# Swapping the two DMA issuers of a matrix-per-sample residual kernel: ScalarE for the loads, SyncE for the stores

## The chip, the core and the metric

The kernel runs on one core of a Trainium2 chip. The metric is the device time of one execution in microseconds (us). Before the change it is 326.86 us, the median of 3 runs (326.13 to 327.13). The profile is one further execution of the same program, taken by the hardware profiler; its span is 325.4 us.

## What is computed

There are 128 samples. Each has a matrix x[b] of 128 channels by 1024 steps, and an index that picks one of eight 128 by 128 weight matrices. The picked matrix, transposed, is multiplied with x[b], and x[b] is added to the product. All numbers are 32-bit floats.

```python
# x: (128, 128, 1024) f32; itok_B_0_7: (128,) int32 in 0..7; L0_cond_weights: (8, 128, 128) f32
def reference(x, itok_B_0_7, L0_cond_weights):
    w = L0_cond_weights[itok_B_0_7]
    return x + jnp.einsum('bct,bcd->bdt', x, w)
```

So 67.11 MB of x are read and 67.11 MB of output are written, beside 0.52 MB of weights and 512 bytes of indices.

## The kernel before

The work goes in 32 tiles of four samples (`NT`, with `G * H = 4`), and a tile in two pairs of samples (`j` counts the 64 pairs). Twelve tiles of x fit into SBUF at once (`SLOTS`, the buffers `x0` to `x11`, 2 MB each); tile i uses buffer i modulo 12. The output is written over x in its buffer and stored from there, so a buffer comes free when its store has landed.

Everything is in one hand-ordered block (`tc.tile_critical()`, line 139). Each engine runs its own list of instructions in the written order, and the lists meet only at semaphores:

- SyncE (line 161 to 169) first loads all eight matrices into `w_all`, then each sample of x by its own DMA of 512 KB, four for a tile. From tile 12 on it waits, before the first load of a tile, until the buffer's earlier store has landed (lines 165 and 167; this is called a slot wait below).
- ScalarE first loads the subjects, that is the 128 indices (line 141). Then it has one store for each tile, of 2 MB, made by `store` (line 130), and before each of them a wait until VectorE has added the tile (`s_added`, line 222). The first tile is stored in two halves, the last tile as one pair and two single samples. ScalarE does no arithmetic in this kernel.
- VectorE clears `zeros`, clamps the indices (lines 153 to 157), and then adds product and x for each pair (line 217, 128 by 2048 elements in one instruction).
- GpSimd (POOL in the profile) loads the indices into registers, sixteen at a time, and copies for each sample the picked matrix out of `w_all` into one of four buffers `w` (line 196). The copy of a pair's first sample also waits until the pair's x has landed and until its PSUM buffer is free.
- TensorE (PE) warms up with products of zeros (line 146) and then makes four products for each pair, two for each sample (line 206), into one of two PSUM buffers `ps`.

`transfer` (line 50) makes each DMA of x and of the output directly, on the hardware queue of the engine that it is given (`QUEUES`, line 47), so the engine in the call settles which queue carries the bytes. A load reads a sample's 512 KB as 32 rows of 16 KB of DRAM; a store of several samples reads two samples' rows together, 8 KB for each partition.

At the end of the block all engines meet on SyncE (its instructions of line 139). A second block (lines 227 to 230) then waits on SyncE for all stores that are still on their way, and ScalarE issues the very last store, sample 127, outside both blocks (line 231), so that the framework's own end of the program waits for that one. Lines 253 and 262 stand for the opening and the closing of the program.

Of the kernel before, what the change touches and what calls it, by code (L numbers as in the profile page):

```python
# [30 lines left out]
G = 2  # L31
H = 2
# [3 lines left out]
SLOTS = 12  # L36
# [5 lines left out]
DMA = 16  # L42
# [7 lines left out]
def transfer(nc, engine, out, in_):  # L50

    later, nc._always_lower_symbolic_ap = nc._always_lower_symbolic_ap, False
    ins, outs = engine.lower_ap_dma(in_), engine.lower_ap_dma(out)
    nc._always_lower_symbolic_ap = later
    return engine.add_instruction(  # L57
        mybir.InstDMACopy(
            name=nc.get_next_instruction_name(),
            engine=engine.engine,  # L60
            ins=ins,
            outs=outs,
            mode="Copy",
            cce_op=ALU.bypass,
            queue=QUEUES[engine.engine],
        )
    )


@with_exitstack  # L70
def kernel(
    ctx: ExitStack,
    tc: tile.TileContext,
    x: bass.AP,
    subjects: bass.AP,
    weights: bass.AP,
    out: bass.AP,
):
    nc = tc.nc
    B, C, T = x.shape  # L80
    S, _, D = weights.shape
    NT = B // (G * H)

    def sbuf(name, *shape, dtype=F32):
        return ctx.enter_context(nc.sbuf_tensor(name, list(shape), dtype)).ap()

    given, near, wrap, index = (
        sbuf(name, 1, B, dtype=I32) for name in ("given", "near", "wrap", "index")
    )
    w_all = sbuf("w_all", C, S, D)  # L90
    ws = [sbuf(f"w{i}", C, 1, D) for i in range(W_SLOTS)]
    zeros = sbuf("zeros", C, N)
    xs = [sbuf(f"x{i}", C, H * G, T) for i in range(SLOTS)]
    ps = [
        ctx.enter_context(nc.psum_tensor(f"ps{i}", [D, G, T], F32)).ap() for i in range(P_SLOTS)
    ]

    s_given = tc.alloc_semaphore("s_given")
    s_wall = tc.alloc_semaphore("s_wall")
    s_index = tc.alloc_semaphore("s_index")  # L100
    s_zeros = tc.alloc_semaphore("s_zeros")
    s_copied = tc.alloc_semaphore("s_copied")
    s_product = tc.alloc_semaphore("s_product")
    s_added = tc.alloc_semaphore("s_added")

    s_pair = [[tc.alloc_semaphore(f"s_pair{i}_{h}") for h in range(H)] for i in range(SLOTS)]


    s_first = tc.alloc_semaphore("s_first")

    def emptied(i, h):

        turns = i // SLOTS
        return (DMA * G + (DMA if h == H - 1 else 0)) * turns

    def loaded(i, q):

        h = q // G
        return s_pair[i % SLOTS][h], emptied(i, h) + DMA * G

    def load(engine, i, q):
        k, h = i % SLOTS, q // G
        transfer(
            nc,
            engine,
            xs[k][:, q, :],
            x[i * H * G + q].rearrange("(a r) t -> a (r t)", r=ROWS),
        ).then_inc(s_pair[k][h], DMA)

    def store(i, q0, q1):  # L130
        k, b = i % SLOTS, i * H * G
        transfer(
            nc,
            nc.scalar,
            out[b + q0 : b + q1].rearrange("g d t -> d g t"),
            xs[k][:, q0:q1, :].rearrange("d (o g) t -> d o (g t)", g=min(G, q1 - q0)),
        ).then_inc(s_first if i == 0 and q1 == G else s_pair[k][(q1 - 1) // G], DMA)

    with tc.tile_critical():  # L139

        nc.scalar.dma_start(given, subjects.rearrange("(o b) -> o b", o=1)).then_inc(s_given, DMA)

        nc.vector.memset(zeros, 0.0).then_inc(s_zeros, 1)  # L143
        nc.tensor.wait_ge(s_zeros, 1)
        for _ in range(IDLE):
            nc.tensor.matmul(  # L146
                ps[P_SLOTS - 1][:, G - 1, :N], zeros[:, :D], zeros, start=True, stop=True
            )

        nc.vector.wait_ge(s_given, DMA)
        nc.vector.tensor_scalar(near, given, -S, S - 1, ALU.max, ALU.min).then_inc(s_index, 1)  # L153
        nc.vector.wait_ge(s_index, 1)
        nc.vector.tensor_scalar(wrap, near, 0, S, ALU.is_lt, ALU.mult).then_inc(s_index, 1)  # L155
        nc.vector.wait_ge(s_index, 2)
        nc.vector.tensor_tensor(index, near, wrap, ALU.add).then_inc(s_index, 1)  # L157
        nc.gpsimd.wait_ge(s_index, 3)


        nc.sync.dma_start(w_all, weights.rearrange("s c d -> c s d")).then_inc(s_wall, DMA)  # L161
        for i in range(NT):
            k = i % SLOTS
            if i == SLOTS:
                nc.sync.wait_ge(s_first, DMA)
            if i >= SLOTS:
                nc.sync.wait_ge(s_pair[k][H - 1], emptied(i, H - 1))
            for q in range(H * G):
                load(nc.sync, i, q)


        for j in range(NT * H):
            i, q0, q1 = j // H, j % H * G, (j % H + 1) * G
            k = i % SLOTS
            p = ps[j % P_SLOTS]

            ahead = j < P_SLOTS
            if ahead:  # L180
                nc.tensor.wait_ge(*loaded(i, q0))
            for q in range(q0, q1):
                b = i * H * G + q
                if b % R == 0:
                    _, subject = nc.values_load_multi_w_load_instructions(
                        index[0:1, b : b + R],
                        engines=[mybir.EngineType.Pool],
                        min_val=0,
                        max_val=S - 1,
                        skip_runtime_bounds_check_because="the index is clamped on the chip above",  # L190
                    )
                if b == 0:
                    nc.gpsimd.wait_ge(s_wall, DMA)
                if not ahead and q == q0:
                    nc.gpsimd.wait_ge(s_added, j - P_SLOTS + 1)
                copy = nc.gpsimd.tensor_copy(  # L196
                    ws[b % W_SLOTS], w_all[:, bass.ds(subject[b % R], 1), :]
                )
                if not ahead and q == q0:
                    copy.wait_op(*loaded(i, q0), "sem-ge")  # L200
            copy.then_inc(s_copied, 1)

            nc.tensor.wait_ge(s_copied, j + 1)
            for q in range(q0, q1):
                for t in range(0, T, N):
                    mm = nc.tensor.matmul(  # L206
                        p[:, q % G, t : t + N],
                        ws[(i * H * G + q) % W_SLOTS][:, 0, :],
                        xs[k][:, q, t : t + N],
                        start=True,  # L210
                        stop=True,
                    )
            mm.then_inc(s_product, 1)

            mine = xs[k][:, q0:q1, :]
            nc.vector.wait_ge(s_product, j + 1)
            nc.vector.tensor_tensor(  # L217
                mine, p, mine, ALU.add
            ).then_inc(s_added, 1)

            if i == 0 or q1 == H * G or i == NT - 1:
                nc.scalar.wait_ge(s_added, j + 1)
                store(i, q0 if i in (0, NT - 1) else 0, q1 - (b == B - 1))

    with tc.tile_critical() as waits:
        for i in range(NT - SLOTS, NT):
            nc.sync.wait_ge(s_pair[i % SLOTS][H - 1], emptied(i + SLOTS, H - 1))
        nc.sync.wait_ge(s_pair[(NT - 1) % SLOTS][0], emptied(NT - 1 + SLOTS, 0) + DMA)  # L230
    last = nc.scalar.dma_start(out[B - 1], xs[(NT - 1) % SLOTS][:, H * G - 1, :])

    tc.add_manual_dep(
        last.ins,
        waits.name,
        mybir.DependencyInfo(mybir.DependencyClass.NoSync, mybir.DependencyReason.SCHED_ONLY),
        reason="the end of the program waits for it",
    )
# [27 lines left out]
```

## Time and profile before

| | |
|---|---|
| median of 3 runs | 326.86 us (326.13 to 327.13) |
| the profiled execution, span | 325.4 us |
| busy: PE, VectorE, GpSimd | 241.1, 147.9, 34.3 us |
| moved by DMA | 134.85 MB, 414 GB/s over the span |
| a product, 128x512 (line 206) | 512 of them, 607 ns each |
| an addition, 128x2048 (line 217) | 64 of them, 2292 ns each |
| a load of x: issue to landing, median | 32.3 us |
| a 2 MB store: issue to landing, median | 47.3 us |
| slot waits of SyncE for stores | 78.5 us, 10 times, the longest 9.8 us |

PE is TensorE, DVE is VectorE, ACT is ScalarE, SP is SyncE; a q behind an engine's name means its sequencer, which issues DMAs and waits. A row of 40 digits cuts the span into equal slices of 8.1 us, and each digit is a busy share in tenths (9 is 90% or more). In the queue table the columns are packets, megabytes, and the time that the packets took as a share of all 16 DMA engines over the span. In a table by stretches, each row gives the stretch, its length, the busy time of PE, weight load, DVE and POOL with the number of instructions, the granted TensorE clock, the busy share of the DMA engines (over 1.00 where packets overlap a little) and GB/s. In a timeline a row gives start, duration, engine, line, operation, what it writes and reads, and how many instructions it covers.

The issue of a DMA is short where its queue has room and lasts until there is room where it has none; the transfer itself goes on after it, and its landing is told by the semaphore.

### The profile page before, as it was taken

The page shows a single profiled execution, that of the slowest core. Times are in us where ns is not written, and L with a number is a line of the kernel's source. Part 1 is how long each engine was busy: PE and PEld are TensorE (multiplying, and loading weights), DVE is VectorE, ACT ScalarE, POOL GpSimd, SP SyncE. Part 2 cuts the span into 40 slices and gives each one's busy share as a digit, 9 for nine tenths or more (in the row PEclk, how much of TensorE's full clock was granted, in tenths as well). Part 3 has the DMA queues.
Part 4 walks back from the last instruction along what each step waited for, and adds up shares of the span by engine and source line. Part 5 has one row for each costly group of instructions (what it writes and reads, how often), then busy time and mean ns, then how long its engine had stood idle before and what let it go on. Part 6 is the DMA issues. An engine that isn't in the chain of part 4 may idle for free.

```text
span 325.4 us, 1606 instructions
## 1 busy us (share of the span) xinstructions
PE 241.1 (74%) x518; PEld 95.2 (29%) x518; DVE 147.9 (45%) x68; POOL 34.3 (11%) x132
## 2 busy tenths in 40 slices
PE   6999988988888888888888888888888689000000
PEld 2444332333333333333333333333333233000000
DVE  1375754555555555454555555554554544200000
POOL 1011111011111111111011111111111010000000
PEclk9999999999999999999999999999999889655555
DMA  6999999999999999999999999999999999999994
GB/s 250 413 418 421 428 425 422 420 428 427 426 421 427 429 415 427 424 431 423 423 435 417 416 432 424 428 417 428 433 419 424 418 437 415 429 425 427 426 428 201
DMA packets 16074, 134.85 MB, mean 414 GB/s; under 512 B 2625, under 2 KB 3650, under 8 KB 3906
## 3 DMA queue, kind: packets, MB, share of 16 engines
q1 hardware_dynamic: 7184, 67.64, 49.7%
q10 hardware_dynamic: 8882, 67.11, 49.1%
q8 instruction: 4, 0.07, 0.1%
q14 instruction: 4, 0.03, 0.0%
HBM read 67.63 MB, written 67.11 MB: 414 GB/s over the span
## 4 chain that ended last, share of the span: by engine, by line
PE 42%; DVE 20%; issue 16%; POOL 4%; DMA 2%; POOLq 1%; SPq 0%
PE ps L206 42%; DVE x L217 20%; POOL w L196 4%; DMA x<-in_x_dram 2%; POOLq L196 1%; SPq L57 0%; SPq L161 0%; POOLq L139 0%; SPq L262 0%; SPq L139 0%
## 5 line engine op out<-in xcount | busy, mean ns | idle before, releaser
L206 PE MATMUL ps<-x,w 128*128 128x512 f32 x512 | 236.1, 607 | 33.6 <-POOL w L196 32.1
L217 DVE TENSOR_TENSOR x<-ps,x 128x2048 f32<-128x2048 f32 x64 | 146.7, 2292 | 129.1 <-PE ps L206 129.1
L206 PEld LDWEIGHTS ps<-x,w 128*128 128x128 f32 x512 | 93.3, 191 | 176.6 <-issue 93.9
L196 POOL COPY w<-w_all 128x128 f32 x128 | 34.1, 296 | 238.0 <-DMA x<-in_x_dram 207.7
L146 PE MATMUL ps<-zeros 128*128 128x512 f32 x6 | 5.0, 992 | 1.7 <-DVE zeros L143 1.7
L146 PEld LDWEIGHTS ps<-zeros 128*128 128x128 f32 x6 | 1.8, 328 | 3.7 <-issue 2.1
L143 DVE MEMSET zeros<- 128x512 f32 x1 | 0.5, 485 | 1.1 <-SPq L139 1.1
L153 DVE TENSOR_SCALAR near<-given 1x128 int32<-1x128 int32 x1 | 0.2, 215 | 0.6 <-DMA given<-in_itok_B_dram 0.6
L157 DVE CUSTOM_DVE_ANT_0 index<-near,wrap 1x256 uint16<-1x256 uint16 x1 | 0.3, 278 | 0.0
L155 DVE TENSOR_SCALAR wrap<-near 1x128 int32<-1x128 int32 x1 | 0.2, 216 | 0.0
L253 POOL MEMSET const-float32-0.0<- 128x1 f32 x1 | 0.1, 99 | 0.2 <-issue 0.2
L253 POOL MEMSET const-bfloat16-1.0<- 128x1 bf16 x1 | 0.1, 102 | 0.0
L253 POOL MEMSET const-uint8-127<- 128x1 uint8 x1 | 0.1, 102 | 0.0
L253 POOL MEMSET const-float32-1.0<- 128x1 f32 x1 | 0.1, 99 | 0.0
## 6 DMA issues: line engine op xcount, KB each, us to landing
x<-in_x_dram SPq DMA_DIRECT2D x128, 512.0 KB, 32.3
out_dram<-x ACTq DMA_DIRECT2D x30, 2048.0 KB, 47.3
out_dram<-x ACTq DMA_DIRECT2D x3, 1024.0 KB, 13.9
out_dram<-x ACTq DMA_DIRECT2D x2, 512.0 KB, 21.1
w_all<-in_L_cond_weights_dram SPq DMA_DIRECT2D x1, 512.0 KB, 4.5
given<-in_itok_B_dram ACTq DMA_DIRECT2D x1, 0.5 KB
```

The costliest lines, as they stand in the source:

```text
L143: nc.vector.memset(zeros, 0.0).then_inc(s_zeros, 1)
L146: nc.tensor.matmul(ps[P_SLOTS - 1][:, G - 1, :N], zeros[:, :D], zeros, start=True, stop=True)
L153: nc.vector.tensor_scalar(near, given, -S, S - 1, ALU.max, ALU.min).then_inc(s_index, 1)
L155: nc.vector.tensor_scalar(wrap, near, 0, S, ALU.is_lt, ALU.mult).then_inc(s_index, 1)
L157: nc.vector.tensor_tensor(index, near, wrap, ALU.add).then_inc(s_index, 1)
L196: copy = nc.gpsimd.tensor_copy(ws[b % W_SLOTS], w_all[:, bass.ds(subject[b % R], 1), :])
L206: mm = nc.tensor.matmul(p[:, q % G, t : t + N], ws[(i * H * G + q) % W_SLOTS][:, 0, :], xs[k][:, q, t : t + N], start=True, stop=True,)
L217: nc.vector.tensor_tensor(mine, p, mine, ALU.add).then_inc(s_added, 1)
L253: nc = _bacc.Bacc("TRN2", target_bir_lowering=False, num_devices=1)
```

## The change

Every DMA is issued by the other one of the two engines. `store`, the load of the subjects and the final store go from ScalarE to SyncE; the load of the matrices and all loads of x go from SyncE to ScalarE, with the waits that belong to them. Sizes, shapes, semaphores, the order within each list and the other three engines are untouched. In the lists of instructions this gives SyncE the subjects, 34 stores with their waits, the meeting of all engines and the final store, and ScalarE the matrices, 128 loads with the slot waits, and the second block's waits.

```diff
@@ store @@
         transfer(
             nc,
-            nc.scalar,
+            nc.sync,
             out[b + q0 : b + q1].rearrange("g d t -> d g t"),
@@ with tc.tile_critical(): @@
-        nc.scalar.dma_start(given, subjects.rearrange("(o b) -> o b", o=1)).then_inc(s_given, DMA)
+        nc.sync.dma_start(given, subjects.rearrange("(o b) -> o b", o=1)).then_inc(s_given, DMA)
...
-        nc.sync.dma_start(w_all, weights.rearrange("s c d -> c s d")).then_inc(s_wall, DMA)
+        nc.scalar.dma_start(w_all, weights.rearrange("s c d -> c s d")).then_inc(s_wall, DMA)
         for i in range(NT):
             k = i % SLOTS
             if i == SLOTS:
-                nc.sync.wait_ge(s_first, DMA)
+                nc.scalar.wait_ge(s_first, DMA)
             if i >= SLOTS:
-                nc.sync.wait_ge(s_pair[k][H - 1], emptied(i, H - 1))
+                nc.scalar.wait_ge(s_pair[k][H - 1], emptied(i, H - 1))
             for q in range(H * G):
-                load(nc.sync, i, q)
+                load(nc.scalar, i, q)
...
             if i == 0 or q1 == H * G or i == NT - 1:
-                nc.scalar.wait_ge(s_added, j + 1)
+                nc.sync.wait_ge(s_added, j + 1)
                 store(i, q0 if i in (0, NT - 1) else 0, q1 - (b == B - 1))
...
     with tc.tile_critical() as waits:
         for i in range(NT - SLOTS, NT):
-            nc.sync.wait_ge(s_pair[i % SLOTS][H - 1], emptied(i + SLOTS, H - 1))
-        nc.sync.wait_ge(s_pair[(NT - 1) % SLOTS][0], emptied(NT - 1 + SLOTS, 0) + DMA)
-    last = nc.scalar.dma_start(out[B - 1], xs[(NT - 1) % SLOTS][:, H * G - 1, :])
+            nc.scalar.wait_ge(s_pair[i % SLOTS][H - 1], emptied(i + SLOTS, H - 1))
+        nc.scalar.wait_ge(s_pair[(NT - 1) % SLOTS][0], emptied(NT - 1 + SLOTS, 0) + DMA)
+    last = nc.sync.dma_start(out[B - 1], xs[(NT - 1) % SLOTS][:, H * G - 1, :])
```

## The prediction

> **What bounds the kernel now.** I read the 40 slices and the queue table of the page first, because they say which resource is full for how long.
>
> ```profile
> span 325.4 us, 1606 instructions
> ...
> PE   6999988988888888888888888888888689000000
> ...
> DMA  6999999999999999999999999999999999999994
> GB/s 250 413 418 421 428 425 422 420 428 427 426 421 427 429 415 427 424 431 423 423 435 417 416 432 424 428 417 428 433 419 424 418 437 415 429 425 427 426 428 201
> ...
> q1 hardware_dynamic: 7184, 67.64, 49.7%
> q10 hardware_dynamic: 8882, 67.11, 49.1%
> q8 instruction: 4, 0.07, 0.1%
> q14 instruction: 4, 0.03, 0.0%
> ```
>
> The 16 DMA engines are full in 38 of 40 slices, while PE is empty in the last six. The shares in the queue table add up to 98.9% of 325.4 us, so the mean DMA engine works 321.8 us and idles 3.6. By its bytes q1 is SyncE's queue (67.11 MB of x and 0.52 of w_all), q10 ScalarE's (all stores). The chain of waits on the page (PE 42%, DVE 20%) ends with the last addition at 278.7 us and does not see the 45 us of stores behind it, so I don't count by it.
>
> Next I read how the two queues share the engines, in the DMA view cut to 60 to 160 us, and how long one issue lasts, by line 57 (minimum, median, maximum in ns).
>
> ```profile
> q1 hardware_dynamic: 2275, 24.79, 58.7%
> q10 hardware_dynamic: 2281, 17.64, 42.0%
> ...
> x<-in_x_dram SPq DMA_DIRECT2D x48, 512.0 KB, 33.1
> out_dram<-x ACTq DMA_DIRECT2D x11, 2048.0 KB, 59.1
> ```
>
> ```profile
> L57 SPq DMA_DIRECT2D x<-in_x_dram x128: 471/1198/4919, 1.5 to 261.1; - x128
> L57 ACTq DMA_DIRECT2D out_dram<-x x34: 556/4733/14475, 14.2 to 300.5; - x34
> ```
>
> The queues take turns, one packet each (2275 against 2281), and loads get more bytes (24.79 against 17.64 MB) only since their packets are larger: on one engine a load is two packets of 16 KB and one semaphore word, a 2 MB store sixteen of 8 KB and one word. So 32/3 KB against 128/17 KB a turn, 1.42; measured 1.41. The median times (1198 and 4733 ns) are far above the minimum (471 and 556): both issuers mostly stand in front of a full queue, and a load waits 33 us in it.
>
> Last the two ends: the timeline of the issuers, and the tail by stretches (the last columns are DMA share and GB/s).
>
> ```profile
> 0.92 0.53 ACTq L141 DMA_DIRECT2D given<-in_itok_B_dram  x1
> 0.96 0.43 SPq L161 DMA_DIRECT2D w_all<-in_L_cond_weights_dram  x1
> ...
> 305.02 0.54 ACTq L231 DMA_DIRECT2D out_dram<-x  x1
> ```
>
> ```profile
> 280.00:316.00 36.00, 0.00 (x0) 0.00 (x0) 0.00 (x0) 0.00 (x0) 0.50 1.01 427
> ...
> 321.00:322.00 1.00, 0.00 (x0) 0.00 (x0) 0.00 (x0) 0.00 (x0) 0.50 0.36 147
> 322.00:323.00 1.00, 0.00 (x0) 0.00 (x0) 0.00 (x0) 0.00 (x0) 0.50 0.06 25
> 323.00:324.00 1.00, 0.00 (x0) 0.00 (x0) 0.00 (x0) 0.00 (x0) 0.50 0.06 25
> ```
>
> At 0.06, one of 16, a single late engine ends the program: its last packet is over at 324.0, the last store's landing is 305.02 + 19.4 = 324.4, and 0.9 us of closing barrier follow.
>
> **The change, part by part.** The sum is made against the profiled 325.4 us; the median of the runs, 326.86, lies 1.46 above it, and I carry that over.
>
> *All 165 data transfers change their issuer.* ScalarE issues w_all and the 128 loads, SyncE 35 stores (the final one, line 231, among them) and the subjects. Sizes, rows and packets stay, so the 98.9% stay: 0 us, as long as no queue runs dry. With one packet each in turn, the share of loads and stores goes with the packets and not with the queue, so 58.7 and 42.0 should stay, with the names swapped. What covers a shift of some per cent: when the last addition ends at 278.7 us, 45 us of stores (19 MB at 427 GB/s) are still queued.
>
> *The cost of an issue.* For 512 KB ScalarE shows 0.54 us (line 231), SyncE 0.47 to 0.61 where nothing blocks. The largest gap in the rows is the first pair, 0.53 against 0.43, so 0.1 us more a load; 129 of them would be 13 us if nothing hid them. What hides them is the queue: in the first 14 us loads land 1.28 us apart and are issued 0.64 apart, later they land 2.1 us apart and are issued 33 us ahead. 0 us, until an issue takes over 1.28.
>
> *The waits.* No wait is added or removed. The slot waits (78.5 us before loads on line 57, ten times) now hold ScalarE; behind them stand only loads, as now. The waits on s_added hold SyncE; behind them only stores, as now. ScalarE has no arithmetic that they could delay.
>
> *The start.* w_all begins at 0.92 instead of 0.96 and may take 0.53 instead of 0.43: from -0.04 to +0.1 us before the first x. I take 0. The subjects move to SyncE; the indices are loaded by POOL until 4.2 us and w_all lands only at 5.4, so 1.2 us cover that.
>
> *The end.* Line 231 no longer needs the hop from SyncE to ScalarE (ScalarE's last store issue ends at 304.5, line 231 starts at 305.0): up to 0.5 us earlier, and nothing gained, since it then lies 19.4 us in the queue. The slot waits after the loop move to ScalarE. On SyncE they and the bookkeeping run from 323.16 (the landing of the last but one store) to 323.95, under the landing at 324.4. Of such a string on ScalarE there is no row. Bounds: no slower, 0; twice as slow, 323.16 + 1.58 = 324.74, 0.32 late. I take 0, as one semaphore instruction of line 262 shows 17 ns on ScalarE and 17 to 28 on SyncE.
>
> *Instruction packets.* They travel on the same 16 engines: four of 16 KB in q8 (48, 115, 184 and 252 us), four of 8 KB in q14 within the span (0.31 us each). The even spacing in q8 fits PE, which has 1036 of the 1606 instructions. With 128 issues gone from SyncE to ScalarE, one packet of 8 KB may move to or from the late engine: -0.31 to +0.31 us; I take 0. The Trainium skill ("Runtime: NRT & Kernel Launch", Instruction fetch mechanics) has every sequencer fetch blocks of 16 KiB through a DMA queue of its own, mostly hidden. By it this term is 0 and the two rivals on the tail lose their cause; the trace has the 16 KB packets but also 8 KB ones, and where the DMA engines are the bound, I hold nothing on them to be hidden.
>
> Sum: 0 us, bounds -0.35 (start and packet) and +0.73 (start, end, packet). Span 325.4, time 326.9, by the bounds 326.5 to 327.6; the three runs lie 0.73 below to 0.27 above their median, so 325.8 to 327.9.
>
> **The rivals.**
> *The share follows the queue (slower).* If q1's 58.7% were q1's privilege, stores would get it. They can't pass what loads deliver, so both would run at some 213 GB/s, no stores would pile up, and the last x would land near the end. Then the last two matrices' work lies open: from the last load's landing (272.0) to the end of the last addition (278.7) are 6.7 us, of which one earlier 2 MB store fills at most 4.9. That adds 1.8 to 6.7 us; the middle, 4.2, gives 331.1. It decides once fewer than 6.7 us of stores (2.9 MB) are queued when the last x lands; now it is 19 MB. Against it: packet sizes explain 1.42 of 1.41. For it: no row has loads in q10. 0.07.
>
> *The tail gets shorter (faster).* From 322.3 to 324.0 one engine works alone. If SyncE's instruction packets and others of q14 fell to it and now fall elsewhere, up to 4 x 0.31 = 1.24 us go, at most the whole 1.7: 325.7 to 325.2. For it: that engine is late by something that the other 15 don't carry. Against: the larger instruction packets, q8's, stay. 0.15.
>
> *The tail gets longer (slower).* The same packets put on the late engine, with ScalarE's string of waits twice as slow: +1.24 + 0.32, so 328.5. 0.12.
>
> *ScalarE can't feed the loads (slower).* With 2.4 us an issue, 128 loads take 307 us, and the 6.7 us of work and 2.5 for the last 1 MB store follow: some 316, still before the stores' end, so it costs only where the queue runs dry in the first 14 us: 1.1 us for each of ten loads, 338. It decides from 1.28 us an issue; the rows have 0.54. 0.02. The Trainium skill ("DMA: Bandwidth & Descriptors", Issuing engine by pattern) names Sync for simple loads and stores, which speaks for this rival; it has no price, and in no row of ScalarE here is an unblocked issue slow.
>
> **How the numbers follow.** 0.3% of 326.86 is 0.98 us, about what a measurement of this kernel can tell from no change. The forecast, 326.9, has 0.64 and lies within it, so 0.64 for the same; faster 0.15 by the shorter tail; slower 0.07 + 0.12 + 0.02 = 0.21. The forecast's own range, 325.8 to 327.9, is widened to 325.5 and 328.9 to take in most of both tails.
>
> **What will show it.** Right: q1 with 67.11 MB and q10 with 67.64, one packet each between 60 and 160 us with 58 to 59% for the loads, 425 to 427 GB/s throughout, DMA queues busy for 98 to 99% of the span, the last addition near 279 us, and a tail of one engine. Wrong: loads under 50% there and additions up to the end (the first rival); a tail at 0.06 that is over a microsecond shorter or longer (the second and third); a DMA share under 0.95 in the first 20 us after 4 us (the fourth); an ACT wait string that ends after the last store's landing (the end).

## The result and the profile after

The changed kernel takes 326.05 us (median of 21 runs, 325.58 to 326.79), the kernel before 326.64 us in the 21 runs beside it. The ratio is 0.998 with a 95% interval of 0.9974 to 0.9986: 0.2% faster, less than the 0.3% that the prediction counted as a difference, but the interval leaves out 1. The profiled execution has a span of 324.4 us, 1.0 less than the one before. That is more than the 0.6 us between the medians: in every execution with both figures the time lies some 1.75 us above its own span, so the span of 325.4 us goes with the time of 327.13, the longest of the first three, and not with their median.

The page of the changed kernel first: span, DMA slices, and the queue table (packets, MB, share of 16 engines).

```profile
span 324.4 us, 1608 instructions
...
DMA  7999999999999999999999999999999999999995
...
q10 hardware_dynamic: 7184, 67.64, 49.8%
q1 hardware_dynamic: 8882, 67.11, 49.3%
q8 instruction: 4, 0.07, 0.1%
q14 instruction: 4, 0.03, 0.0%
```

The queues have changed places, and nothing else has moved: the shares add up to 99.2% of 324.4 us, which is 321.8 us of work for a mean DMA engine, as before. The 1.0 us came out of the idle 3.6. The DMA view from 60 to 160 us and the issues of line 57 (minimum, median, maximum ns):

```profile
q10 hardware_dynamic: 2276, 24.82, 58.8%
q1 hardware_dynamic: 2280, 17.63, 42.0%
```

```profile
L57 ACTq DMA_DIRECT2D x<-in_x_dram x128: 478/1255/4269, 1.4 to 260.1; - x128
L57 SPq DMA_DIRECT2D out_dram<-x x34: 539/4730/13972, 13.9 to 299.4; - x34
```

Loads have 58.8% on q10 as they had 58.7% on q1, one packet each in turn. The issues last as long on the one engine as on the other. The two ends, by the timeline and by stretches:

```profile
0.93 0.43 ACTq L161 DMA_DIRECT2D w_all<-in_L_cond_weights_dram  x1
...
0.97 0.36 SPq L141 DMA_DIRECT2D given<-in_itok_B_dram  x1
...
304.13 0.38 SPq L231 DMA_DIRECT2D out_dram<-x  x1
```

```profile
320.00:321.00 1.00, 0.00 (x0) 0.00 (x0) 0.00 (x0) 0.00 (x0) 0.50 0.68 279
321.00:322.00 1.00, 0.00 (x0) 0.00 (x0) 0.00 (x0) 0.00 (x0) 0.50 0.29 119
322.00:323.00 1.00, 0.00 (x0) 0.00 (x0) 0.00 (x0) 0.00 (x0) 0.50 0.07 29
323.00:324.00 1.00, 0.00 (x0) 0.00 (x0) 0.00 (x0) 0.00 (x0) 0.50 0.00 0
```

Where before one engine was still at work through 322 to 324 (0.06 in both rows), it is done by 323. To see how much of the 1.0 us is that, I summed the bytes of all packets over time in both traces. The changed kernel is 0.18 us ahead when 1 MB is carried, 0.18 when 134.3 of 134.85 MB are carried, and 1.05 at the last byte. So the middle gives nothing, the start 0.18, the tail 0.87.

One more thing can be read from the packets. On one DMA engine a packet begins 3 or 4 ns before the packet ahead of it ends, so the string of packets of each of the 16 engines can be followed through the trace (from 27 to 311 us; where two engines' ends coincide, two strings may be exchanged). In the kernel before, 15 strings take 311 ns for 8 KB of a store and 616 ns for 16 KB of a load. One takes 314 and 620, 1% more, as long as the compute engines work, and 311 after that. And on that same string lies an 8 KB instruction packet, at 125.4 us; the data packet behind it takes 582 ns instead of 311. In the changed kernel such a packet comes at 114.4 us, on a string that is not slow. That gave the theory for the experiments: the slow engine is the late one at the end, SyncE's instruction packets travel on it, and with 128 issues gone SyncE fetches none while the loads run. Behind 311 us, where all engines carry stores at 311 ns, the strings can't be told apart with certainty; that the slow one is the one that ends last is a guess at this point.

### The profile page after: what moved, and what is told of

It is laid out like the page before. It is cut to its first block, busy times and chain, and to the rows that moved or that the text cites. A ratio compares the mean times of both kernels' runs of the same rounds, so it can differ in the third digit from the quotient of the medians.

```text
span 324.4 us, 1608 instructions
## 1 busy us (share of the span) xinstructions
PE 240.2 (74%) x518; PEld 94.5 (29%) x518; DVE 147.9 (46%) x68; POOL 34.3 (11%) x132
## 2 busy tenths in 40 slices
DMA packets 16074, 134.85 MB, mean 416 GB/s; under 512 B 2625, under 2 KB 3650, under 8 KB 3906
## 4 chain that ended last, share of the span: by engine, by line
PE 41%; DVE 20%; issue 18%; POOL 4%; DMA 2%; POOLq 1%; ACTq 0%; SPq 0%
PE ps L206 41%; DVE x L217 20%; POOL w L196 4%; DMA x<-in_x_dram 2%; POOLq L196 1%; ACTq L57 0%; ACTq L161 0%; ACTq L262 0%; SPq L139 0%
```

## The experiments

Each is timed beside the kernel before on the same chip, in 4 to 12 executions, one of which is profiled; the groups of experiments ran on five different chips. A time below is a median, the ratio is against the kernel before.

**The two kernels again.** No edit.

> The kernel before, unchanged, as a control. If the 0.2% between the two kernels is real, this run lies within 0.1% of the kernel before (ratio 0.999 to 1.001). Theory 'late engine': which DMA engine is late depends on who issues, so its tail again shows one engine alone for over 1.2 us and a last packet about 2.5 us behind the mean of the 16. Rival 'chance': the 2.5 us of the first profile were that one execution's, and this profile's tail may as well be like that of the changed kernel (about 1.7).

> The changed kernel, unchanged. 'Late engine': 0.997 to 0.999 again, the first 0.5 MB about 0.1 to 0.2 us earlier than in the kernel before, and a tail about 0.9 us shorter than in the control's profile. 'Chance': a ratio that covers 1, or a tail as long as the control's.

Measured: 326.58 us, 1.000 (0.9991 to 1.0009), and 325.91 us, 0.9977 (0.9967 to 0.9987). The gain is real. The start is not part of it: the repeated changed kernel carries its first 4 MB 0.02 us before the first profile of the kernel before, the repeated kernel before 0.18 us before it. The last packet is 2.17 us behind the mean of the 16 engines' ends in the repeated kernel before (2.46 in its first profile) and 1.21 in the repeated changed one (1.66). The tail of the repeated kernel before, in its last two stretches with work:

```profile
322.00:323.00 1.00, 0.00 (x0) 0.00 (x0) 0.00 (x0) 0.00 (x0) 0.50 0.06 25
323.00:324.00 1.00, 0.00 (x0) 0.00 (x0) 0.00 (x0) 0.00 (x0) 0.50 0.03 12
```

Again one engine alone, until 323.5.

**Fewer instructions on TensorE.** The lines for the warm-up products are left out here:

```diff
...
-            for q in range(q0, q1):
-                for t in range(0, T, N):
+            for q in range(q0, q0 + 1):
+                for t in range(0, N, N):
```

> The kernel before, but TensorE makes only one of the four products of each pair (three quarters of the products are left out), after warm-up products that cover all of both PSUM buffers. All DMAs of data stay. TensorE goes from 1036 to about 144 instructions, so q8's four 16 KB instruction packets should be gone. 'Late engine': the lateness at the end comes from instruction packets that fell on a few engines; without q8 the last engine is at most about 1.2 us behind the mean instead of 2.5, and the time falls by 0.3 to 0.5% (1.0 to 1.6 us). Rival 'drift': an engine is late for other reasons (stalls at the start, slower turns), and time and tail stay within 0.3 us.

> The changed kernel with the same three quarters of the products left out. 'Late engine': it falls as well, by 0.1 to 0.3% against the changed kernel (its tail has 0.8 us less to lose), and what is left between the two kernels without q8 is the start, 0.1 to 0.2 us. Rival 'the issuer's own instruction packets': the two kernels without q8 stay 0.5 us apart, as with it.

Measured: 325.72 us, 0.997 (0.9959 to 0.998), and 325.47 us, 0.9956 (0.9943 to 0.9969). One of q8's four packets stayed (at 153.6 us), so the first number is a little smaller than expected, 0.9 us instead of 1.0 to 1.6, and the last packet of the kernel before is still 1.64 us behind the mean instead of 1.2. "Drift" alone is out, "late engine" alone too: q8's packets lie on four different strings, and what the missing 750 instructions changed on the late one is the slowness itself (2.0 us over the run instead of 2.6). The 0.25 us between the two kernels lies between what the two theories gave, and the two intervals overlap, so it decides nothing; which string ends last can't be told here, as a second engine ends only some 0.5 us before the last one in both traces.

**More instructions, on the one issuer or the other.** Four increments behind each load, or fifteen behind each store, of semaphores that nothing waits for. These are the two edits of the kernel before; in the changed kernel the engines are exchanged:

```diff
                 load(nc.sync, i, q)
+                for n in range(4):
+                    nc.sync.sem_inc(s_pad[n], 1)
...
                 store(i, q0 if i in (0, NT - 1) else 0, q1 - (b == B - 1))
+                for n in range(15):
+                    nc.scalar.sem_inc(s_pad[n % 8], 1)
```

> The kernel before, with four increments of an unused semaphore behind each load on SyncE: 512 more instructions there, about four more instruction packets of 8 KB. Theory 'slow engine': one DMA engine runs about 1% slow while the compute engines work (2.5 us over the run in both profiles of the kernel before), and SyncE's instruction packets travel on that same engine; each costs it 0.31 us and 0.27 more on the packet behind. Then four more give +2.3 us, ratio 1.005 to 1.009, and a tail of one engine that is about 2 us longer. Rival 'any packet does' (no tie between SyncE and the slow engine): within 0.3 us, as each other engine has 1.2 us or more to spare. Rival 'slower issue': a lower DMA share in the first 20 us.

> The kernel before, with fifteen increments of unused semaphores behind each store on ScalarE (510 more instructions there). 'Slow engine': ScalarE's packets travel on an engine that has time to spare, so the four more packets cost it 2.3 us under the slow engine's lateness: within 0.4 us of the kernel before. 'Any packet does': the same time as with the padding on SyncE.

> The changed kernel with four increments behind each load, now on ScalarE. 'Slow engine': 0.997 to 0.999 of the kernel before, as without the padding or at most 0.3 us more. 'Slower issue' or 'any packet does': as much slower as with the same padding on SyncE in the kernel before (+2.3 us).

> The changed kernel with fifteen increments behind each store, now on SyncE. 'Slow engine': the changed kernel's gain is gone and more: its SyncE packets fall on the slow engine again, +1.7 to +2.3 us against the changed kernel, so 1.003 to 1.006 of the kernel before. 'Any packet does': within 0.4 us of the changed kernel.

Measured: on SyncE 330.44 us, 1.0115 (1.0099 to 1.013), in the kernel before, and 329.15 us, 1.0074 (1.006 to 1.0088), in the changed one. On ScalarE 327.47 us, 1.0025 (1.0015 to 1.0034), in the kernel before, and 326.75 us, 1.0005 (0.9994 to 1.0017), in the changed one. So +3.9 and +3.2 us on SyncE, +0.9 and +0.8 on ScalarE, whichever of them issues the loads. The order is the one that "slow engine" gave, but all four cost more than it allowed. "Slower issue" is out: of the 134.85 MB, the kernel before padded on SyncE has carried 134.3 MB at 319.9 us, and the two unpadded profiles of that kernel at 319.9 and 319.7; all that it loses comes behind that. The tails of the kernel before, padded on SyncE and padded on ScalarE:

```profile
323.00:324.00 1.00, 0.00 (x0) 0.00 (x0) 0.00 (x0) 0.00 (x0) 0.50 0.06 25
324.00:325.00 1.00, 0.00 (x0) 0.00 (x0) 0.00 (x0) 0.00 (x0) 0.50 0.06 25
325.00:326.00 1.00, 0.00 (x0) 0.00 (x0) 0.00 (x0) 0.00 (x0) 0.50 0.06 25
326.00:327.00 1.00, 0.00 (x0) 0.00 (x0) 0.00 (x0) 0.00 (x0) 0.50 0.07 29
```

```profile
323.00:324.00 1.00, 0.00 (x0) 0.00 (x0) 0.00 (x0) 0.00 (x0) 0.50 0.07 29
324.00:325.00 1.00, 0.00 (x0) 0.00 (x0) 0.00 (x0) 0.00 (x0) 0.50 0.06 25
325.00:326.00 1.00, 0.00 (x0) 0.00 (x0) 0.00 (x0) 0.00 (x0) 0.50 0.00 0
```

Both have eight instruction packets in q14 instead of four. With the padding on SyncE, four of them after 27 us lie on the slow string in each of the two kernels; with the padding on ScalarE, four lie together on another string. So the guess holds: what is put on the slow string comes out as the time of one engine alone at the end. The sizes come out of the strings. Slowness is the extra time of a string's packets from 27 to 311 us, those behind instruction packets left out (where two strings were exchanged, both parts are added):

```text
kernel           instructions  slowness of     SyncE's packets
                 in the trace  the slow one    on it, at us
before               1606        2.58          125.4
before, again        1606        2.49          123.5
changed              1608        2.41          none
changed, again       1608        2.44          none
before, few           858        2.02          125.0
changed, few          860        1.67          none
before, pad ScalarE  2116        3.44          124.1
before, pad SyncE    2118        3.31          57.9 110.9 166.8 244.2
changed, pad SyncE   2118        3.33          43.4 112.3 209.4 287.3
changed, one SyncE   1710        2.52          184.4
```

No other string has much more than 0.2. In the changed kernel, four packets of 0.31 us and 0.25 to 0.28 for each packet behind them make 2.3, the larger slowness 0.9: 3.2 us, as measured. In the kernel before, the packets behind SyncE's four take 0.27 to 0.44 us longer. On ScalarE only the slowness is left, 0.9 in the kernel before, as measured (the profile there is of the longest of ten executions, 328.27 us, so that agreement is rough). This second term I had not expected: slowness grows with the instructions in the trace, whichever engine runs them.

**One packet back, and nothing else.** The question that was left: is SyncE's one packet the whole 0.6 us? The two edits of the changed kernel:

```diff
                 store(i, q0 if i in (0, NT - 1) else 0, q1 - (b == B - 1))
+                for n in range(3):
+                    nc.sync.sem_inc(s_pad[n], 1)
```

```diff
                 load(nc.scalar, i, q)
+                if q < 3:
+                    nc.scalar.sem_inc(s_pad[q], 1)
```

> The changed kernel with three increments of unused semaphores behind each store on SyncE: its list has 158 instructions there instead of 56 (the kernel before has 161), so one 8 KB packet on SyncE as there. Theory 'one packet': 0.31 us for it, 0.27 for the packet behind it, and some 0.1 to 0.2 for 102 more instructions on the slow engine's drift: the gain of the swap is gone, 0.999 to 1.001 of the kernel before, and the last engine again over 2 us behind the mean. Rival 'another effect of the swap': it stays at 0.9975 to 0.9985.

> The changed kernel with 96 increments on ScalarE, three of them among the four loads of a tile (251 instructions there instead of 155): one packet more on ScalarE's engine, none on SyncE. 'One packet': only the drift's 0.1 to 0.2 us, so 0.998 to 0.999. 'Instructions as such': the same as with the increments on SyncE.

Measured: 326.76 us, 1.000 (0.9991 to 1.0009), with the increments on SyncE; 325.90 us, 0.9976 (0.9966 to 0.9987), with them on ScalarE. The executions don't overlap: 326.21 to 327.19 on SyncE, 325.73 to 326.18 on ScalarE. The packet is seen in the DMA view of the kernel with the increments on SyncE, from 184 to 185 us:

```profile
q10 hardware_dynamic: 20, 0.20, 46.6%
q1 hardware_dynamic: 22, 0.18, 44.5%
q14 instruction: 1, 0.01, 1.9%
```

It lies on the slow string, and the packet behind it takes 0.27 us more. The tails in halves of a microsecond, SyncE's first, ScalarE's second:

```profile
322.50:323.00 0.50, 0.00 (x0) 0.00 (x0) 0.00 (x0) 0.00 (x0) 0.50 0.06 25
323.00:323.50 0.50, 0.00 (x0) 0.00 (x0) 0.00 (x0) 0.00 (x0) 0.50 0.02 8
```

```profile
322.00:322.50 0.50, 0.00 (x0) 0.00 (x0) 0.00 (x0) 0.00 (x0) 0.50 0.06 25
322.50:323.00 0.50, 0.00 (x0) 0.00 (x0) 0.00 (x0) 0.00 (x0) 0.50 0.00 0
```

The last packet is 1.77 us behind the mean of the engines' ends on SyncE, less than the 2 expected, and 1.15 on ScalarE. One packet undoes the swap; nearly as many instructions on the other engine undo nothing.

**Three tries that missed.** The first cuts the final store so that one DMA engine has nothing of its larger part:

```diff
-    last = nc.sync.dma_start(out[B - 1], xs[(NT - 1) % SLOTS][:, H * G - 1, :])
+    most = D - D // 16
+    last = [
+        nc.sync.dma_start(out[B - 1, r], xs[(NT - 1) % SLOTS][r, H * G - 1, :])
+        for r in (slice(0, most), slice(most, D))
+    ]
...
```

> A try to beat both: the changed kernel, but the final store (sample 127, 128 rows of 4 KB) is cut into one of 120 rows and one of 8. 120 rows go by 15, so if the cut spares the slow engine, that engine has 8 packets of 159 ns less at the end (1.27 us), the others up to one more. 'Slow engine', spared: no engine alone at the end, the last packet 0.6 to 1.0 us earlier, ratio 0.995 to 0.9965 of the kernel before. If another engine is spared (which one the slow one is, the trace doesn't tell): the same tail or 0.16 us more, 0.9975 to 0.9985.

> The same cut in the kernel before. 'Slow engine', spared: its late engine was 1.2 us behind the second latest (324.00 against 322.75), so up to 1.2 us less, ratio 0.996 to 0.9975, and the gap to the changed kernel with the same cut shrinks to 0 to 0.4 us. Otherwise 0.999 to 1.001.

Measured: 326.39 us, 0.999 (0.998 to 0.9999), and 327.18 us, 1.0019 (1.0011 to 1.0028): 0.3 to 0.6 us worse than without the cut, where 0 to 0.16 was expected for an engine not spared. In both traces the engine that ends last carries a packet of the short store too (0.16 us; the rest of the loss is not explained). So that engine, the slow one by the padded runs, is one of the eight that the 8 rows went to, and was not the one spared. The Trainium skill ("DMA: Bandwidth & Descriptors", Why a DMA increments its semaphore by 16 and not by 1) has a DMA over k engines use the lowest-numbered k; by that the slow one is among the first eight. The same page (Latency and other measured facts) calls engines 7 and 15 usually slower than the rest: 15 is out here, 7 is not, and the cause that it guesses at, descriptor rings of GpSimd, has nothing to work on in this kernel, where GpSimd issues no DMA.

The second balances the two lists of instructions, and was meant to leave neither issuer a packet:

```diff
-                load(nc.sync, i, q)
+                load(nc.scalar if i < SLOTS else nc.sync, i, q)
```

(with w_all on ScalarE as well; in the other one the two engines are exchanged)

> The kernel before, but w_all and the loads of the first 12 tiles are issued by ScalarE, ahead of its stores; SyncE keeps the other 80 loads. The program's list has then 112 instructions on SyncE instead of 161 (a packet of 8 KB holds 128 of 64 bytes, by the padded kernels: 512 more gave four packets). Theory 'SyncE's packet on the slow engine': the 8 KB packet at 125 us is gone, nothing else is lost as the DMA queues never run dry, and the time falls by 0.5 to 0.7 us, to the changed kernel's (ratio 0.9975 to 0.9985). Rival 'the order of loads and stores': with stores behind 48 loads on one queue the DMA engines run dry near 60 us, or the last additions end near the end of the stores, and the time is over the kernel before's. Rival 'another effect of the swap': within 0.1% of the kernel before.

> The mirror: SyncE issues the subjects, w_all, the loads of the first 12 tiles and the stores (105 instructions), ScalarE the other 80 loads (106). 'SyncE's packet': no 8 KB packet of either issuer, so the same as the changed kernel or 0.1 us less, since ScalarE's packet lay on an engine with time to spare: 0.997 to 0.9985, and within 0.1% of the other split, whichever engine issues what.

Measured: 328.18 us, 1.0044 (1.0031 to 1.0058), and 328.06 us, 1.0036 (1.0023 to 1.0048). The edit brought a cost of its own: the first 48 loads now go ahead of all stores, and loads alone are carried more slowly. The first of the two by stretches:

```profile
20.00:50.00 30.00, 30.00 (x72) 13.22 (x71) 19.72 (x10) 4.79 (x18) 1.00 1.01 410
...
70.00:160.00 90.00, 82.05 (x183) 35.16 (x182) 52.53 (x23) 11.72 (x44) 0.96 1.01 426
```

410 GB/s against 426 over some 45 us more are 1.7 us; measured are 1.3 and 1.4. And the packet is not gone, as the queue table of each of the two shows, with one packet more than in the kernel before:

```profile
q14 instruction: 5, 0.04, 0.0%
```

So a list of 112 instructions or fewer still brings a packet, against what was expected. In the first of the two one comes at 254.3 us, on the slow string, and the packet behind it takes 1028 ns instead of 616. These runs say nothing on what the swap gained.

The third loads w_all as eight DMAs on the engine of the stores, beside the first loads of x:

```diff
-        nc.scalar.dma_start(w_all, weights.rearrange("s c d -> c s d")).then_inc(s_wall, DMA)
+        for n in range(S):
+            transfer(
+                nc,
+                nc.sync,
+                w_all[:, n, :],
+                weights[n].rearrange("(a r) d -> a (r d)", r=C // DMA),
+            ).then_inc(s_wall, DMA)
...
-                    nc.gpsimd.wait_ge(s_wall, DMA)
+                    nc.gpsimd.wait_ge(s_wall, DMA * S)
```

> The changed kernel, but w_all is loaded by SyncE as eight DMAs of one matrix each (reads of 4 KB in a row instead of 512 bytes), while ScalarE begins at once with x. The 1024 packets of 512 bytes (27 ns each, 1.7 us on each engine) become 128 of 4 KB; at the 159 ns of a 4 KB store packet that is 1.3 us on each engine: up to 0.4 us less, ratio 0.9965 to 0.998 of the kernel before. If writing to eight partitions makes a packet cost as much as eight of 512 bytes (216 ns), or the matrices land so late that the first products wait, there is no gain: 0.9975 to 0.999.

Measured: 328.00 us, 1.004 (1.0027 to 1.0054). The changed kernel moves 411 GB/s from 4 to 8 us and 415 from 8 to 14; this one:

```profile
4.00:8.00 4.00, 2.28 (x4) 0.54 (x2) 0.00 (x0) 0.00 (x0) 1.00 0.99 305
8.00:14.00 6.00, 0.00 (x0) 0.00 (x0) 0.00 (x0) 0.00 (x0) 0.56 1.03 361
```

The DMA engines are full and move less: up to 14 us a 16 KB packet of x, four rows, takes 744 ns in the median instead of 640, and one of w_all 176 for 4 KB. Why the packets of x take longer beside them is not shown. No version beat the changed kernel.

## Why the prediction was right and wrong

*The bound, the share, the issue, the waits: right.* The same 321.8 us of DMA work, 58.8% and 42.0% with the queues exchanged, 425 GB/s in the middle, and the middle gives nothing. So the rival by which the share follows the queue is out, and so is the one by which ScalarE can't feed the loads.

*The start: right at 0.* The 0.1 us more that I allowed for an issue on ScalarE is not there: w_all takes 0.43 us on either engine, and the subjects 0.36 on SyncE against 0.53 on ScalarE.

*The end: right at 0.* Line 231 is issued earlier and its 19.2 us in the queue hide that. The string of waits takes 0.9 us on ScalarE (322.14 to 323.02) against 0.8 on SyncE, and is over before the last landing at 323.37.

*The instruction packets: here it failed.* I took 0 for a packet that "may move to or from the late engine", and bounded the term at 0.31 us, one packet by its own duration. Measured: the packet that the swap takes off the slow engine is worth 0.31 us itself and 0.27 more on the data packet behind it, 0.58 together; the medians differ by 0.6, and putting such a packet back takes the gain away again (1.000 against 0.9976). The sign could have been found too: the rows of the tail showed one engine that is late at the end, and which sequencer's packet lies on the slow string can be followed in the trace before. That engine bounds the kernel, and the step from "the 98.9% stay" to 0 us goes by the mean of the 16. The rival with the shorter tail had the mechanism, and its price of 1.24 to 1.7 us was too high, because the three other packets of q14 lie on other engines. At 0.2% the gain stayed under the 0.3% that the chances counted. That 326.05 still lies inside the forecast's range is owed to the width of the range, not to this term.

*The Trainium skill's rule* ("Runtime: NRT & Kernel Launch", Instruction fetch mechanics), by which fetching instructions is mostly hidden, would make this term 0. It doesn't hold here: on the DMA engine that ends last the packet costs 0.58 us.

What stays open is why that one engine runs 1% slow while the compute engines work, and whether it does so without the profiler's records: it can be seen in the profiles alone.

## What to carry to other kernels

In this kernel, which keeps its DMA engines full, the end is set by the one engine that is latest, not by their mean: look at the stretches in which the DMA share is 1 in 16. Whatever lies on that engine counts in full, instruction packets too, and a long list of instructions on SyncE put them there. On ScalarE the list of the loads cost nothing that shows, and 510 instructions more 0.8 to 0.9 us, against 3.2 to 3.9 on SyncE. Which of the two issues loads and which stores made no other difference.

## What the runs showed of the hardware

- An issuer's instruction packets of 8 KB keep to one DMA engine: ScalarE's four (44.7, 113.8, 210.0 and 286.2 us in the kernel before padded on it) lie on one string, SyncE's on the slow one, in traces of all five chips. The four of 16 KB in q8 lie on four different ones.
- An instruction packet costs its engine more than its own 0.31 us: the data packet behind it takes 0.18 to 0.66 us longer.
- One DMA engine's slowness goes with the number of instructions in the trace: 1.7 to 2.0 us with 860, 2.4 to 2.6 with 1606, 3.3 to 3.4 with 2118, and none from 280 to 311 us, while only stores run. What the cause is was not tried; the profiler's own records are one possibility.
- Loads alone are carried at 410 GB/s (the first split, 20 to 50 us), loads and stores together at 425 and stores alone at 427 (the kernel before).
